# Moving one aggregation step, making M later, and giving the last pair its own end in a GCN and graph-attention kernel

## The chip, the cores and the metric

The kernel runs on one core of one Trainium2 chip. The metric is device time in microseconds (us). Before the change the median of three runs is 2903.5 us (2902.86 to 2904.16). Engine names follow the profile: PE is TensorE, DVE is VectorE, ACT is ScalarE, POOL is GpSimd, SP is SyncE, whose queue issues all DMAs here.

## The reference

There are 64 graphs with 256 nodes and 512 features, all in fp32. Layer 0 is a three-layer GCN with a residual and a layernorm; layer 1 is an attention that gates each node's value vector by a softmax over the nodes of its graph.

```python
def _gcn_layer(x, adj, W, b):
    return adj @ (x @ W) + b                      # per graph
h = relu(_gcn_layer(x, adj, W1, b1)); h = relu(_gcn_layer(h, adj, W2, b2))
x = layernorm(x + _gcn_layer(h, adj, W3, b3))
q, k = split(x @ Wqk, 2); v = x @ Wv
w = mask / sqrt(512) * sum(q * (adj @ (k * mask)), axis=-1)
x = layernorm(x + softmax(w over nodes)[:, :, None] * v)
```

## The kernel before, in words

**Pairs.** Two graphs make a pair, so there are 32 pairs. Nodes are split in two halves of 128 (`h`), features in four chunks of 128 (`c`).

**Seven products.** Every large multiplication apart from the aggregation is done with seven block products in place of eight. `seven` (L96 to L131) fixes their order: 1, 7, 6, 2, 5, 3, 4. Products 1, 6, 5 and 3 accumulate one after another in the same PSUM bank x, product 7 and then 4 in bank v, and 2 has its own bank y. Between them ACT copies the bank out (L103 after 1, L112 after 6, L120 after 5) and DVE adds a bank and a copy into a result block (L62). So product 6 may not start before the copy after 1 is done, product 5 not before the copy after 6, product 3 not before the copy after 5, and product 4 not before DVE's add "c22", which reads the copy after 5 and bank v.

**Sums for the products.** The products need sums of blocks. `a_sums` builds four from one operand on POOL (L65): first S[2] (for product 7), then S[0] (for 5), S[1] (for 6, made from S[0]), S[3] (for 3, made from S[1]). `b_sums` (L87 to L90) does it for the other operand: on DVE for the weights, on POOL for T and for M.

**Front of a pair (F).** `support` (L231) multiplies activations by W with seven products; `aggregate` (L252) multiplies by the adjacency in four steps of four matmuls, one for each feature chunk in the order 2, 3, 0, 1, and ACT evicts each with ReLU (L255). This is done for W1 and W2, then `support` for W3. After the first `support` the transposed x of the next pair is loaded (L70); the plain x of this pair is loaded after the second aggregation (L80).

**Back of a pair (B).** `adj_times` (L284) applies the adjacency (first gather), the residual and the layernorm follow: ACT makes the masked xm (L385), DVE normalises r (L387) and transposes it in 32x32 blocks (L390); the result goes to DRAM (L393) and comes back with four DMAs (L395) as x1T, which completes the transpose. A second gather multiplies adjacency by xm (L284 again, sums on POOL). Then `attention(g)` for each of the two graphs: seven products (L412) of x1T and its sums (POOL, L65) with Wv and with M = Wq Wk^T side by side, 512 columns wide, and the scores on DVE (L416). The text calls these seven products together the double product.

**Making M.** `make_m` loads Wq, Wk and Wv (L181 to L186), multiplies them in four rows of 16 matmuls (L192, copied by ACT L195) and builds the sums mv_T on POOL (L87 to L90).

**Finish of a pair (E).** Softmax of both graphs together: two PE transposes (L305), maximum (L307), exponential on ACT with an activation table load (L310), two transposes back (L319), then gating (L446), bn_stats and aggregate (L453, L457), square root (L294, another table load), normalisation (L462) and the output DMAs, one per graph (L465).

**Order of the work.** Nothing is reordered by a scheduler: each engine runs its instructions as the program issues them. F, B and E are generators; `run` advances them by a string, one letter for each step. Iteration i runs F of pair i, B of pair i-1 and E of pair i-2. `ORDER` is that string for i of 1 and more; iteration 0 uses "FB" six times; the last pair's E runs alone at the end. Buffers with few copies matter: S has 11, v (attention result) 2, x, r, gt, x1T and xT one each, PSUM 8 banks.

Of the kernel before, what the change touches and what calls it, by code (L numbers as in the profile page):

```python
# [9 lines left out]
FP = mybir.dt.float32  # L10
AF = mybir.ActivationFunctionType
# [9 lines left out]
def gcn_then_graph_attention(ctx: ExitStack, tc: tile.TileContext, xT, xN, adjT, mask, W1, b1, W2, b2, W3, b3,  # L21
# [33 lines left out]
    def bank(shape=(P, G, N)):  # L55
        return psum.tile(list(shape), FP, name="ps", tag="ps")
# [4 lines left out]
    def add(o, a, b):  # L61
        nc.vector.tensor_tensor(o, a, b, op=OP.add)  # L62

    def padd(o, a, b, op=OP.add):
        nc.gpsimd.tensor_tensor(o, a, b, op=op)  # L65
# [134 lines left out]
        yield  # L200


    def a_sums(blk, part=None):


        S = [pool.tile([P, 2, G, P], FP, name="S", tag="S", bufs=11) for _ in range(4)]
        sub = OP.subtract

        def first():
            padd(S[2], blk(0, 0), blk(1, 0), sub)  # L210

        def rest():
            padd(S[0], blk(1, 0), blk(1, 1))
            padd(S[1], S[0], blk(0, 0), sub)

        def last():
            padd(S[3], blk(0, 1), S[1], sub)
# [55 lines left out]
    def t_sums(B):  # L273
        Ts = [pool.tile([P, G, HD], FP, name="T", tag="T", bufs=4) for _ in range(4)]
        b_sums((B[0][0], B[0][1], B[1][0], B[1][1]), Ts, nc.gpsimd)
        return Ts

    def adj_times(aS, B, Ts, c11, c12, c21, c22, plus=None):

        mov = {1: B[0][0], 2: B[1][0], 3: B[1][1], 4: Ts[3], 5: Ts[0], 6: Ts[1], 7: Ts[2]}  # L280

        def mm(n, ps, first):
            for g in range(G):
                nc.tensor.matmul(ps[:, g], lhsT=aS[n][:, g], rhs=mov[n][:, g], start=(first and g == 0),  # L284
                                 stop=(g == G - 1), skip_group_check=True)
        yield from seven(mm, (P, G, HD), c11, c12, c21, c22, plus=plus)

    def row_stats(st, src):
        nc.vector.bn_stats(st, src)

    def inv_std(mvt):

        sd = small.tile([P, NH, G], FP, name="sd")
        nc.scalar.activation(sd, mvt[:, :, :, 1], AF.Sqrt, bias=eps)  # L294
        rs = small.tile([P, NH, G], FP, name="rs")
        nc.vector.reciprocal(rs, sd)
        nb = small.tile([P, NH, G], FP, name="nb")
        nc.vector.scalar_tensor_tensor(nb, mvt[:, :, :, 0], -1.0, rs, op0=OP.mult, op1=OP.mult)
        return rs, nb

    def softmax_rows(w):

        pw = bank((G, N))
        for h in range(NH):
            nc.tensor.transpose(pw[:, h * P:(h + 1) * P], w[:, h, :], ident)  # L305
        nmax = small.tile([G, 1], FP, name="nmax")
        nc.vector.tensor_reduce(nmax, pw, AX.X, OP.max, negate=True)  # L307
        e = small.tile([G, N], FP, name="e", bufs=1)
        tot = small.tile([G, 1], FP, name="tot")
        nc.scalar.activation(e, pw, AF.Exp, bias=nmax, accum_out=tot)  # L310
        rtot = small.tile([G, 1], FP, name="rtot")
# [4 lines left out]
    def softmax_cols(sm):  # L316
        ps = bank((P, NH, G))
        for h in range(NH):
            nc.tensor.transpose(ps[:, h, :], sm[:, h * P:(h + 1) * P], ident[:G, :G])  # L319
        s = small.tile([P, NH, G], FP, name="s", bufs=2)  # L320
        nc.vector.tensor_copy(s, ps)
        return s

# [27 lines left out]
        C = yield from steps  # L351
        return C, aS, x, nxt, nS

    def back(i, C, aS, x):
        Ts = t_sums(C)
        r = pool.tile([P, G, NH, D], FP, name="r", bufs=1)
        xb = lambda h, j: x[:, :, h, j * HD:(j + 1) * HD]
# [23 lines left out]
        tr = pool.tile([P, 4, 32, NH, 2, 2, G], FP, name="tr", tag="gt", bufs=1)  # L381
        x1T = pool.tile([P, P, NH, 2, 2, G], FP, name="x1T", bufs=1)
        for h in range(NH):
            for g in range(G):
                nc.scalar.activation(xm[:, g, h, :], r[:, g, h, :], AF.Identity, scale=mrs[:, h, g:g + 1],  # L385
                                     bias=mnb[:, h, g:g + 1])
                nc.vector.tensor_scalar(r[:, g, h, :], r[:, g, h, :], rs[:, h, g:g + 1], nb[:, h, g:g + 1],  # L387
                                        op0=OP.mult, op1=OP.add)
# [3 lines left out]
        via = dram.tile([4, P, D], FP, name="via")  # L392
        nc.sync.dma_start(via.rearrange("q p e -> p q e"), tr.rearrange("p q j h k c g -> p q (j h k c g)"))  # L393
        for q in range(4):
            nc.sync.dma_start(x1T[q * 32:(q + 1) * 32].rearrange("p (a j) h k c g -> p a (j h k c g)", a=4),  # L395
                              via[q].rearrange("(a i) e -> i a e", a=4))
        yield
        xmb = [[xm[:, :, h, j * HD:(j + 1) * HD] for j in range(2)] for h in range(2)]
        Ts = t_sums(xmb)
# [6 lines left out]
        def attention(g):  # L406
# [12 lines left out]
            def c22(ps, t):  # L419
# [5 lines left out]
        yield from adj_times(aS, xmb, Ts, lambda y, t: add(gb(0, 0), y, t), lambda x: nc.scalar.copy(gb(0, 1), x),  # L425
                             lambda v, t: add(gb(1, 0), v, t), lambda v, t: add(gb(1, 1), v, t))
        if i + 2 < NPAIR:
            aTs[i + 2] = load_adj(i + 2)
        src, first, rest, last = a_sums(lambda h, k: x1T[:, :, h, k].rearrange("p n c g -> p c g n"))
        first()  # L430
        rest()
        last()
# [2 lines left out]
            yield from attention(g)  # L435
        return r, vs, w

    def finish(i, prev):

        r, vs, w = prev  # L440
        sm = softmax_rows(w)
        yield
        s = softmax_cols(sm)
        for g in range(G):
            for h in range(NH):
                nc.vector.scalar_tensor_tensor(vs[g][:, h, :], vs[g][:, h, :], s[:, h, g:g + 1], r[:, g, h, :],  # L446
                                               op0=OP.mult, op1=OP.add)
        yield
        st = small.tile([P, NH, G, 6], FP, name="st")
        mvt = small.tile([P, NH, G, 2], FP, name="mvt")  # L450
        for g in range(G):
            for h in range(NH):
                nc.vector.bn_stats(st[:, h, g], vs[g][:, h, :])  # L453
                yield
        for g in range(G):
            for h in range(NH):
                nc.vector.bn_aggr(mvt[:, h, g], st[:, h, g])  # L457
        rs, nb = inv_std(mvt)
        yield
        for g in range(G):  # L460
            for h in range(NH):
                nc.scalar.activation(vs[g][:, h, :], vs[g][:, h, :], AF.Identity, scale=rs[:, h, g:g + 1],  # L462
                                     bias=nb[:, h, g:g + 1])
# [23 lines left out]
    for i in range(NPAIR + 1):  # L487
        gens = {}
        if i < NPAIR:
            aT = aTs[i]  # L490
            gens["F"] = front(i, xTs, xS, aT)
        if i == 0:
            gens["B"] = make_m()
        else:
            gens["B"] = back(i - 1, *state)
        if prev is not None:
            gens["E"] = finish(i - 2, prev)
        res = run(ORDER.replace(" ", "") if i else "FB" * 6, **gens)
# [42 lines left out]
```

## Time and profile before

| what | value |
|---|---|
| median of three runs | 2903.5 us |
| the profiled execution's own time | 2903.94 us |
| its span, first to last instruction | 2902.1 us |
| mean granted TensorE clock | 0.995 |
| busy, DVE / ACT / POOL | 39% / 32% / 49% |
| one iteration in the steady state (from one long "issue" piece of the chain to the next) | 88.31 us |

The profiled execution took 1.84 us more than its span. A page of the profile gives busy times by engine, the span in 40 slices, and groups of instructions by line; the timeline lists instructions in order of time with the start, the duration, the form, and in brackets the idle time of the engine before it and what ended it. Matmuls of fp32 appear as two records for each instruction (a "x8" is four matmuls), and their listed durations overlap, so the starts are what counts.

### The profile page before, as it was taken

What the parts mean: (1) busy time and instruction counts of PE and PEld (TensorE: products, weight loads), DVE (VectorE), ACT (ScalarE), POOL (GpSimd) and SP (SyncE); (2) the same over time, 40 slices, a digit from 0 to 9 for tenths busy, and PEclk for the clock granted to TensorE, in tenths of its full rate; (3) what the DMA queues carried; (4) which work ended last, traced back from release to release, by engine and by line L of the source; (5) the groups of instructions that cost most, each with busy time, mean ns of one, the idle gap of its engine ahead of it and who ended that gap; (6) DMA issues with size and microseconds to landing.
All of it is one profiled execution on the core that took longest, in us unless ns stands there. A gap on an engine that the chain in (4) does not pass through costs nothing.

```text
span 2902.1 us, 29670 instructions
## 1 busy us (share of the span) xinstructions
PE 2828.6 (97%) x11264; PEld 2174.2 (75%) x11264; DVE 1123.4 (39%) x2318; ACT 934.1 (32%) x1510; POOL 1432.1 (49%) x1130
## 2 busy tenths in 40 slices
PE   7999999999999999999999999999999999999995
PEld 6877777777777777777777777777777777777773
DVE  1243334443344433344433444433444333444334
ACT  1323333322333332333223333323332333332232
POOL 2644554354554455553545544545534455435452
PEclk9999999999999999999999999999999999999998
DMA  4211222212222112222122221122221122221111
GB/s 150 66 41 54 66 80 80 60 43 66 72 80 80 44 51 66 80 80 73 39 64 66 80 80 51 44 66 80 80 80 41 54 66 81 80 60 45 56 58 58
DMA packets 64046, 193.10 MB, mean 67 GB/s; under 512 B 5792, under 2 KB 8992, under 8 KB 55712
## 3 DMA queue, kind: packets, MB, share of 16 engines
q1 hardware_dynamic: 63904, 191.19, 21.1%
q8 instruction: 90, 1.47, 0.2%
q14 instruction: 52, 0.43, 0.0%
HBM read 124.06 MB, written 67.11 MB: 66 GB/s over the span
## 4 chain that ended last, share of the span: by engine, by line
PE 65%; issue 17%; POOL 14%; ACT 1%; DMA 1%; DVE 1%; SPq 0%; POOLq 0%; ACTq 0%
PE ps L231 27%; PE ps L412 25%; POOL S L65 8%; PE ps L284 7%; PE ps L252 6%; POOL T L88 2%; POOL T L89 1%; POOL T L87 1%; POOL T L90 1%; ACT hT L255 1%; PE ps L192 1%; DMA w<-in_W 0%; PE ps L319 0%; PE ps L305 0%; DMA wkT<-in_WkT 0%
## 5 line engine op out<-in xcount | busy, mean ns | idle before, releaser
L231 PE MATMUL ps<-w_T,S 128*128 128x256 f32 x2304 | 548.8, 381 | 1.4 <-DVE w_T L87 1.1
L231 PEld LDWEIGHTS ps<-w_T,S 128*128 128x128 f32 x2304 | 433.7, 191 | 106.2 <-issue 51.0
L252 PE MATMUL ps<-aT,sup 128*128 128x256 f32 x2048 | 467.6, 379 | 0.0
L65 POOL TENSOR_TENSOR S<-hT 128x512 f32<-128x512 f32 x128 | 162.4, 1269 | 601.1 <-ACT hT L255 601.1
L252 PEld LDWEIGHTS ps<-aT,sup 128*128 128x128 f32 x2048 | 389.2, 190 | 66.0 <-issue 14.8
L62 DVE TENSOR_TENSOR sup<-ps,tmp 128x512 f32<-128x512 f32 x288 | 198.7, 690 | 509.4 <-PE ps L231 262.6
L412 PE MATMUL ps<-mv_T,S 128*128 128x512 f32 x768 | 367.1, 601 | 27.3 <-POOL S L65 27.3
L65 POOL TENSOR_TENSOR tmp<-tmp,x 128x512 f32<-128x512 f32 x96 | 120.3, 1268 | 485.9 <-ACT tmp L120 295.2
L62 DVE TENSOR_TENSOR v<-ps,tmp 128x512 f32<-128x512 f32 x128 | 88.5, 692 | 692.7 <-PE ps L412 692.7
L255 ACT ACTIVATE hT<-ps,b 128x512 f32<-128x512 f32 x256 | 175.3, 685 | 392.3 <-PE ps L252 392.3
L112 ACT COPY tmp<-ps 128x512 f32<-128x512 f32 x224 | 131.2, 586 | 496.9 <-PE ps L231 219.6
L412 PEld LDWEIGHTS ps<-mv_T,S 128*128 128x128 f32 x768 | 140.7, 190 | 187.9 <-issue 115.3
L103 ACT COPY tmp<-ps 128x512 f32<-128x512 f32 x224 | 129.8, 580 | 410.5 <-PE ps L231 235.9
L120 ACT COPY tmp<-ps 128x512 f32<-128x512 f32 x224 | 131.1, 585 | 374.5 <-PE ps L412 185.3
L412 PE MATMUL ps<-v,x1T 128*128 128x512 f32 x512 | 240.9, 593 | 2.8 <-DMA x1T<-via 2.8
L231 PE MATMUL ps<-w,hT 128*128 128x256 f32 x1024 | 241.9, 379 | 0.0
L231 PEld LDWEIGHTS ps<-w,hT 128*128 128x128 f32 x1024 | 194.6, 190 | 49.7 <-issue 22.2
L284 PE MATMUL ps<-T,aS 128*128 128x256 f32 x768 | 203.4, 388 | 2.1 <-POOL T L87 1.4
L231 PE MATMUL ps<-w,S 128*128 128x256 f32 x768 | 186.4, 386 | 1.5 <-ACT tmp L120 1.5
L231 PEld LDWEIGHTS ps<-w,S 128*128 128x128 f32 x768 | 140.6, 190 | 47.2 <-issue 25.7
L412 PEld LDWEIGHTS ps<-v,x1T 128*128 128x128 f32 x512 | 141.3, 295 | 41.8 <-issue 3.6
L65 POOL TENSOR_TENSOR x<-x,b3b 128x512 f32<-128x512 f32 x128 | 172.1, 1373 | 0.0
(96 smaller groups left out, 3869.8 us busy)
## 6 DMA issues: line engine op xcount, KB each, us to landing
xT<-in_xT SPq DMA_DIRECT2D x32, 1024.0 KB, 4.9
x<-in_xN SPq DMA_DIRECT2D x32, 1024.0 KB, 6.5
via<-tr SPq DMA_DIRECT2D x32, 1024.0 KB, 4.3
x1T<-via SPq DMA_DIRECT2D x128, 256.0 KB, 4.7
out<-v SPq DMA_DIRECT2D x64, 512.0 KB, 3.6
aT<-in_adjT SPq DMA_DIRECT2D x32, 512.0 KB, 3.6
w<-in_W SPq DMA_DIRECT2D x9, 256.0 KB, 5.2
wqT<-in_WqT SPq DMA_DIRECT2D x4, 256.0 KB, 6.1
```

Source lines behind the costliest of these rows:

```text
L62: nc.vector.tensor_tensor(o, a, b, op=OP.add)
L65: nc.gpsimd.tensor_tensor(o, a, b, op=op)
L87: eng.tensor_tensor(Ts[2], B[3], B[1], op=sub)
L88: eng.tensor_tensor(Ts[0], B[1], B[0], op=sub)
L103: nc.scalar.copy(t1, x)
L112: nc.scalar.copy(u, x)
L120: nc.scalar.copy(q, x)
L231: nc.tensor.matmul(ps[:, g], lhsT=src[n][:, c, g], rhs=w[n][:, c], start=(first and g == 0 and c == 0), stop=(g == G - 1 and c == 1), skip ...
L252: nc.tensor.matmul(ps[:, g], lhsT=C[k][c // 2][:, g, (c % 2) * P:(c % 2 + 1) * P], rhs=aT[:, k, g], start=(g == 0 and k == 0), stop=(g == ...
L255: nc.scalar.activation(hT[c // 2][:, c % 2], ps, AF.Relu, bias=b[:, c:c + 1])
L284: nc.tensor.matmul(ps[:, g], lhsT=aS[n][:, g], rhs=mov[n][:, g], start=(first and g == 0), stop=(g == G - 1), skip_group_check=True)
L412: nc.tensor.matmul(ps, lhsT=src[n][:, c, g], rhs=mv[n][:, c], start=(first and c == 0), stop=(c == 1), skip_group_check=True)
```

## The change

1. `ORDER` is rewritten. In every steady iteration one F step, the fourth step of the second aggregation (chunk 1), moves from behind product 7 to ahead of it: PE's order was "1, 7, aggregation step, 6" and is now "1, aggregation step, 7, 6". The later F steps are spread anew between the products of the two graphs, and E's last steps come a place earlier, so that both output DMAs are issued ahead of the load of x.
2. Iteration 0 runs twelve F steps first and then F and B in turn, so the rows of M stand between the products of the second `support`, not of the first. On SP's queue the load of the next pair's xT then stands ahead of the loads of Wq, Wk and Wv.
3. The last pair has its own end. Its r is transposed by 16 TensorE transposes into four PSUM banks, which DVE (first half) and ACT (second half) copy to x1T; the two DRAM passes are gone. Its a_sums run on DVE. The second gather (G) and the first graph's products (M) are interleaved as "GMGMGMGMGGGMMM". The softmax and the finish are done for each graph by itself: the first graph's between the second graph's products, the second's at the end. The steps of E of the pair before are spread over this end by a string of their own.

The rest is parameters: `a_sums` takes an engine, `inv_std`, `softmax_rows`, `softmax_cols` and `finish` take a number or list of graphs. The call of `a_sums` for x1T stands ahead of the second gather in the program, but its instructions are issued where they were.

```diff
-    def a_sums(blk, part=None):
+    def a_sums(blk, eng=nc.gpsimd):
...
-            padd(S[2], blk(0, 0), blk(1, 0), sub)
+            eng.tensor_tensor(S[2], blk(0, 0), blk(1, 0), op=sub)
...
-    def back(i, C, aS, x):
+    def back(i, C, aS, x, end):
...
+        if end:
+            x1T = pool.tile([P, 2, 2, G, N], FP, name="x1T", bufs=1)
+            x1b = lambda h, k: x1T[:, k, :, :, h * P:(h + 1) * P]
+            for h, g in hg:
+                apply(h, g)
+            Ts = t_sums(xmb)
+            for h, g in hg:
+                pt = bank((P, 2, 2, P))
+                for c in range(DC):
+                    nc.tensor.transpose(pt[:, c // 2, c % 2], r[:, g, h, c * P:(c + 1) * P], ident)
+                (nc.scalar.copy if h else nc.vector.tensor_copy)(x1T[:, :, :, g, h * P:(h + 1) * P], pt)
+        else:
...
+        src, first, rest, last = a_sums(x1b, nc.vector if end else nc.gpsimd)
+        if end:
+            first()
+            rest()
+            last()
+            one = attention(0)
+            for k in "GMGMGMGMGGGMMM":
+                next(gather if k == "G" else one)
+                yield
...
+            tail = finish(i, (r, vs, w), [0])
+            for _ in attention(1):
+                next(tail, None)
+                yield
+            for _ in tail:
+                pass
+            for _ in finish(i, (r, vs, w), [1]):
+                pass
+            return
+        yield from gather
...
-    ORDER = ("F E F" + " B F" + " B F E" * 5 + " B F B F F B B F F B F" + " B F" * 3 + " B F E" * 4 + " E B" +
-             (" B F" * 2 + " B" + " B F" * 3 + " B") * 2)
+    ORDER = ("F E F" + " B F" + " B F E" * 5 + " B F B F F B B F F B F" + " B F"*3 + " B F E"*3 + " B E F E" + " B F E B B F B B F B F B" + " B F B B F B B F B F B")
+    START = "F" * 12 + "F B" * 6
+    END = "E B B B E" + "B" * 5 + "B E" * 10
...
-    for _ in finish(NPAIR - 1, prev):
-        pass
```

More of the change, by code (lines that the diff above doesn't have):

```diff
@@ L209, in first @@
         def first():
-            padd(S[2], blk(0, 0), blk(1, 0), sub)
+            eng.tensor_tensor(S[2], blk(0, 0), blk(1, 0), op=sub)
         def rest():
-            padd(S[0], blk(1, 0), blk(1, 1))
-            padd(S[1], S[0], blk(0, 0), sub)
+            eng.tensor_tensor(S[0], blk(1, 0), blk(1, 1), op=OP.add)
+            eng.tensor_tensor(S[1], S[0], blk(0, 0), op=sub)
         def last():
-            padd(S[3], blk(0, 1), S[1], sub)
+            eng.tensor_tensor(S[3], blk(0, 1), S[1], op=sub)
         return {1: blk(0, 0), 2: blk(0, 1), 4: blk(1, 1), 5: S[0], 6: S[1], 7: S[2], 3: S[3]}, first, rest, last
@@ L286, in adj_times, with inv_std, softmax_rows @@
         yield from seven(mm, (P, G, HD), c11, c12, c21, c22, plus=plus)
[L288 to L293, printed above, removed]
+    def inv_std(mvt, n=G):
+        sd = small.tile([P, NH, n], FP, name="sd")
         nc.scalar.activation(sd, mvt[:, :, :, 1], AF.Sqrt, bias=eps)
-        rs = small.tile([P, NH, G], FP, name="rs")
+        rs = small.tile([P, NH, n], FP, name="rs")
         nc.vector.reciprocal(rs, sd)
-        nb = small.tile([P, NH, G], FP, name="nb")
+        nb = small.tile([P, NH, n], FP, name="nb")
         nc.vector.scalar_tensor_tensor(nb, mvt[:, :, :, 0], -1.0, rs, op0=OP.mult, op1=OP.mult)
         return rs, nb
-    def softmax_rows(w):
-        pw = bank((G, N))
+    def softmax_rows(w, gs):
+        n = len(gs)
+        pw = bank((n, N))
         for h in range(NH):
-            nc.tensor.transpose(pw[:, h * P:(h + 1) * P], w[:, h, :], ident)
-        nmax = small.tile([G, 1], FP, name="nmax")
+            nc.tensor.transpose(pw[:, h * P:(h + 1) * P], w[:, h, gs[0]:gs[0] + n], ident)
+        nmax = small.tile([n, 1], FP, name="nmax")
         nc.vector.tensor_reduce(nmax, pw, AX.X, OP.max, negate=True)
-        e = small.tile([G, N], FP, name="e", bufs=1)
-        tot = small.tile([G, 1], FP, name="tot")
+        e = small.tile([n, N], FP, name="e", bufs=1)
+        tot = small.tile([n, 1], FP, name="tot")
         nc.scalar.activation(e, pw, AF.Exp, bias=nmax, accum_out=tot)
-        rtot = small.tile([G, 1], FP, name="rtot")
+        rtot = small.tile([n, 1], FP, name="rtot")
         nc.vector.reciprocal(rtot, tot)
@@ L314, in softmax_rows, with softmax_cols @@
         return e
-    def softmax_cols(sm):
-        ps = bank((P, NH, G))
+    def softmax_cols(sm, gs):
+        n = len(gs)
+        ps = bank((P, NH, n))
         for h in range(NH):
-            nc.tensor.transpose(ps[:, h, :], sm[:, h * P:(h + 1) * P], ident[:G, :G])
-        s = small.tile([P, NH, G], FP, name="s", bufs=2)
+            nc.tensor.transpose(ps[:, h, :], sm[:, h * P:(h + 1) * P], ident[:n, :n])
+        s = small.tile([P, NH, n], FP, name="s", bufs=2)
         nc.vector.tensor_copy(s, ps)
@@ L380, in back, with apply @@
         xm = pool.tile([P, G, NH, D], FP, name="xm", tag="x", bufs=1)
[L381 to L388, printed above, removed]
+        def apply(h, g):
+            nc.scalar.activation(xm[:, g, h, :], r[:, g, h, :], AF.Identity, scale=mrs[:, h, g:g + 1],
+                                 bias=mnb[:, h, g:g + 1])
+            nc.vector.tensor_scalar(r[:, g, h, :], r[:, g, h, :], rs[:, h, g:g + 1], nb[:, h, g:g + 1],
+                                    op0=OP.mult, op1=OP.add)
+        hg = [(h, g) for h in range(NH) for g in range(G)]
+        xmb = [[xm[:, :, h, j * HD:(j + 1) * HD] for j in range(2)] for h in range(2)]
+        if end:
[10 more added lines that the diff above has]
+        else:
+            tr = pool.tile([P, 4, 32, NH, 2, 2, G], FP, name="tr", tag="gt", bufs=1)
+            x1T = pool.tile([P, P, NH, 2, 2, G], FP, name="x1T", bufs=1)
+            x1b = lambda h, k: x1T[:, :, h, k].rearrange("p n c g -> p c g n")
+            for h, g in hg:
+                apply(h, g)
                 for k in range(2):
@@ L391, in back @@
                                         r[:, g, h, k * HD:(k + 1) * HD].rearrange("p (c q j) -> p c q j", c=2, q=4))
[L392 to L399, printed above, removed]
+            via = dram.tile([4, P, D], FP, name="via")
+            nc.sync.dma_start(via.rearrange("q p e -> p q e"), tr.rearrange("p q j h k c g -> p q (j h k c g)"))
+            for q in range(4):
+                nc.sync.dma_start(x1T[q * 32:(q + 1) * 32].rearrange("p (a j) h k c g -> p a (j h k c g)", a=4),
+                                  via[q].rearrange("(a i) e -> i a e", a=4))
+            yield
+            Ts = t_sums(xmb)
         yield
@@ L424, in attention @@
                              lambda ps, t: add(v[:, 1, :], ps, t), c22)
-        yield from adj_times(aS, xmb, Ts, lambda y, t: add(gb(0, 0), y, t), lambda x: nc.scalar.copy(gb(0, 1), x),
-                             lambda v, t: add(gb(1, 0), v, t), lambda v, t: add(gb(1, 1), v, t))
+        gather = adj_times(aS, xmb, Ts, lambda y, t: add(gb(0, 0), y, t), lambda x: nc.scalar.copy(gb(0, 1), x),
+                           lambda v, t: add(gb(1, 0), v, t), lambda v, t: add(gb(1, 1), v, t))
+        src, first, rest, last = a_sums(x1b, nc.vector if end else nc.gpsimd)
[7 more added lines that the diff above has]
+                yield
+            for _ in gather:
+                pass
+            for _ in one:
+                pass
+            tail = finish(i, (r, vs, w), [0])
+            for _ in attention(1):
+                next(tail, None)
+                yield
+            for _ in tail:
+                pass
+            for _ in finish(i, (r, vs, w), [1]):
+                pass
+            return
+        yield from gather
         if i + 2 < NPAIR:
             aTs[i + 2] = load_adj(i + 2)
-        src, first, rest, last = a_sums(lambda h, k: x1T[:, :, h, k].rearrange("p n c g -> p c g n"))
         first()
@@ L436, in back, with finish @@
         return r, vs, w
-    def finish(i, prev):
+    def finish(i, prev, gs=range(G)):
         r, vs, w = prev
-        sm = softmax_rows(w)
+        n = len(gs)
+        sm = softmax_rows(w, gs)
         yield
-        s = softmax_cols(sm)
-        for g in range(G):
+        s = softmax_cols(sm, gs)
+        for k, g in enumerate(gs):
             for h in range(NH):
-                nc.vector.scalar_tensor_tensor(vs[g][:, h, :], vs[g][:, h, :], s[:, h, g:g + 1], r[:, g, h, :],
+                nc.vector.scalar_tensor_tensor(vs[g][:, h, :], vs[g][:, h, :], s[:, h, k:k + 1], r[:, g, h, :],
@@ L447, in finish @@
                                                op0=OP.mult, op1=OP.add)
         yield
-        st = small.tile([P, NH, G, 6], FP, name="st")
-        mvt = small.tile([P, NH, G, 2], FP, name="mvt")
-        for g in range(G):
+        st = small.tile([P, NH, n, 6], FP, name="st")
+        mvt = small.tile([P, NH, n, 2], FP, name="mvt")
+        for k, g in enumerate(gs):
             for h in range(NH):
-                nc.vector.bn_stats(st[:, h, g], vs[g][:, h, :])
+                nc.vector.bn_stats(st[:, h, k], vs[g][:, h, :])
@@ L454, in finish @@
                 yield
-        for g in range(G):
+        for k in range(n):
             for h in range(NH):
-                nc.vector.bn_aggr(mvt[:, h, g], st[:, h, g])
-        rs, nb = inv_std(mvt)
+                nc.vector.bn_aggr(mvt[:, h, k], st[:, h, k])
+        rs, nb = inv_std(mvt, n)
         yield
-        for g in range(G):
+        for k, g in enumerate(gs):
             for h in range(NH):
-                nc.scalar.activation(vs[g][:, h, :], vs[g][:, h, :], AF.Identity, scale=rs[:, h, g:g + 1],
-                                     bias=nb[:, h, g:g + 1])
+                nc.scalar.activation(vs[g][:, h, :], vs[g][:, h, :], AF.Identity, scale=rs[:, h, k:k + 1],
+                                     bias=nb[:, h, k:k + 1])
@@ L494, in gcn_then_graph_attention @@
         else:
-            gens["B"] = back(i - 1, *state)
+            gens["B"] = back(i - 1, *state, i == NPAIR)
         if prev is not None:
             gens["E"] = finish(i - 2, prev)
-        res = run(ORDER.replace(" ", "") if i else "FB" * 6, **gens)
+        order = START if i == 0 else ORDER if i < NPAIR else END
+        res = run(order.replace(" ", ""), **gens)
         if i > 0:
```

## The prediction

> **What bounds the kernel.** First the page: busy times, then the slices.
>
> ```profile
> PE 2828.6 (97%) x11264; PEld 2174.2 (75%) x11264; DVE 1123.4 (39%) x2318; ACT 934.1 (32%) x1510; POOL 1432.1 (49%) x1130
> ...
> PE   7999999999999999999999999999999999999995
> ```
>
> PE is the bound in every slice but the first and the last. The change removes no matmul, so it can only win what PE idles: in the steady state, at the start, at the end. Second, the timeline of PE and then POOL in one steady iteration (start, duration, form, idle time before it):
>
> ```profile
> 1196.01 1.88 PE L412 MATMUL ps<-v,x1T 128*128 128x512 f32 x4
> 1198.72 1.98 PE L412 MATMUL ps<-mv_T,S 128*128 128x512 f32 x4 [0.82 <-POOL S L65]
> 1200.54 1.89 PE L252 MATMUL ps<-aT,sup 128*128 128x256 f32 x8
> 1202.27 1.98 PE L412 MATMUL ps<-mv_T,S 128*128 128x512 f32 x4
> ```
>
> ```profile
> 1195.25 1.27 POOL L65 TENSOR_TENSOR S<-hT 128x512 f32<-128x512 f32 x1 [12.26 <-ACT hT L255]
> 1196.48 4.12 POOL L65 TENSOR_TENSOR S<-x1T 128x512 f32<-128x512 f32 x2
> 1200.68 1.52 POOL L65 TENSOR_TENSOR S<-S,x1T 128x512 f32<-128x512 f32 x1
> ```
>
> The four PE rows are product 1, product 7, the aggregation step and product 6. Product 7 waits for S[2], POOL's first sum of x1T; this is the largest wait of an iteration (27.3 us in all, 33 times). Counted from starts it is 1198.72 - 1196.01 - 1.72 (a product back to back) = 0.99. Note when S[1] is done: 1200.68 + 1.52 = 1202.20, and product 6, which reads it, starts at 1202.27.
>
> Third, the first 30 us on PE:
>
> ```profile
> 11.64 3.75 PE L231 MATMUL ps<-w_T,S 128*128 128x256 f32 x8 [1.11 <-DVE w_T L87]
> 21.36 6.28 PE L192 MATMUL ps<-wkT,wqT 128*128 128x128 f32 x32 [5.96 <-DMA wkT<-in_WkT]
> 29.20 3.73 PE L192 MATMUL ps<-wkT,wqT 128*128 128x128 f32 x32
> ```
>
> PE idles 5.96 us for the weights of M. The first two rows are also slow: product 7 takes 3.55 from start to end against 1.73 later, and the first row of M 6.1 against 3.57. The rows become fast at 26.4, 5.0 us into unbroken work. (The stage table gives a granted clock of 1.00 here and 0.52 for 2847 to 2853; its records come late, so I go by the starts of rows.)
>
> Fourth, the end:
>
> ```profile
> 2840.53 2.08 PE L284 MATMUL ps<-xm,aT 128*128 128x256 f32 x4 [6.13 <-ACT xm L385]
> 2846.74 0.37 SPq L393 DMA_DIRECT2D via<-tr  x1
> 2851.14 1.74 SPq L395 DMA_DIRECT2D x1T<-via  x4
> 2857.83 2.06 PE L412 MATMUL ps<-v,x1T 128*128 128x512 f32 x4 [2.80 <-DMA x1T<-via]
> 2863.63 1.98 PE L412 MATMUL ps<-mv_T,S 128*128 128x512 f32 x4 [1.55 <-POOL S L65]
> 2889.28 2.74 DVE L446 SCALAR_TENSOR_TENSOR v<-v,s,r 128x512 f32<-128x512 f32 x4
> 2895.50 2.93 ACT L462 ACTIVATE v<-v,nb,rs 128x512 f32<-128x512 f32 x4 [0.49 <-DVE nb L298]
> ```
>
> With no front beside it, the double product starts only when x1T is back from DRAM (2857.83), waits for POOL's sums, and after its last matmul (2886.28) both graphs' softmax and finish stand alone, 15.82 us.
>
> **Part 1, the moved step: nothing.** POOL's order of instructions is unchanged, and its chain starts at the same event: ACT's eviction of the aggregation's second step (1195.25). So S[1] is still ready at 1202.20. New PE order: product 1 at 1196.01, the step at 1197.73, product 7 at 1199.45 (S[2], ready at 1198.67, no longer holds it), done at 1201.17. Product 6 then waits for S[1] until 1202.25. Before, it started at 1202.27. The wait of 0.99 goes and one of 1.08 comes, one product later. I take -0.02 x 31 = -0.6 us, with ends of -3 and +3 (0.1 an iteration, the size of a restart after a wait in these rows).
>
> The steps spread anew: every product keeps at least one other product (1.72) between itself and the copy it needs, which takes about 0.9 (0.2 to start, 0.58 to copy, 0.06 back). The products 4 now have three between. DVE and ACT do the same work within a few us. T's sums on POOL start some 3.4 us later (product 3 of the front is two places later), at about 1230.7, and are needed at 1241.3: hidden. On SP both outputs now precede the load of x: the issue moves from 1196.35 to about 1198.8, it lands 6.5 later, and POOL reads x at 1210.41: hidden, with 5 us to spare.
>
> **Part 2, M later: -6.3.** The time to compare is the first product of pair 1, at 87.62. After: product 6 follows product 7 at 15.19. With the 5.0 us of above the slow stretch ends at 16.6, and the 1.5 us of it beyond 15.19 cost half, 0.8: 17.7. Products 2, 5, 3, 4 take 4 x 1.73, and 0.93 for the copy ahead of product 3 (as at 63.82): 25.6. Aggregation 6.91: 32.5. Products 1, 7 and 6 with 0.3 for S[1]: 37.9. Four rows of M (3.57 each) with three products: 57.4. Now POOL's sums for M come later against the front by one product: they start 0.87 after the last row and take 9.47, as before (44.24 to 53.71), until 67.7. PE has product 4, aggregation and product 1 until 67.7, then waits for the third support's S[2] and S[1], queued on POOL behind them: product 6 at 71.6 (3.89 after, as at 57.60). This wait is 2.2 in place of 0.4. From there 9.74 as before: 81.3. The eight loads for M now queue on SP behind the load of xT, which waits for product 4 (25.8). It lands at about 30.7, and at the 0.68 us between landings in this trace the eight are in by 36.1, 1.8 before the first row. If that cover goes, each us late is a us lost. Ends: -7 (no slow stretch beyond 15.19) to -1 (loads up to 5 late).
>
> **Part 3, the last end: -9.3.**
> - Up to the layernorm (xm starts at 2839.66): E's bn_stats no longer stand among DVE's residual adds; one (0.66) was on the path, and its neighbours: -0.95, so 2838.7.
> - r follows ACT tile by tile (0.85 behind, 0.7 apart), then 16 transposes. The trace has no 128x128 transpose; the nearest rows are L305, two columns wide and warm (0.109 each), and L192, slow (0.213 a record, and 0.427 with two records). I take 0.213, since one transpose is one record in L305 and the clock is low: 2840.15 to 2843.55. Ends 1.7 and 6.9 in all. The copies to x1T cost 0.58 and 0.69 each (L112, L62), DVE's four sums 0.69 each as in L88, up to 1.60 where POOL works beside (L87 at 9.89); S[2] by 2846 at worst, needed at about 2849: hidden.
> - Second gather 7 x 0.86 and first graph 7 x 1.72 interleaved: 18.1. Slow clock: no row tells whether transposes count as work that ends the slow stretch, so I count its 5.0 us from halfway, 2841.9; 3.4 us of the block are slow and cost 1.7 (ends 0 and 9.0, all of it slow). Waits: 0.9 twice, where product 3 follows 5 directly, and 0.5 where DVE's c11 of the first graph waits for a v buffer, whose output DMA is issued only after ACT's normalisation in this stretch (2.7 to land); queued behind it on DVE is the gather's c22, for which product 4 waits. End at 2865.6; the second graph started at 2873.32: -7.7.
> - Second graph: 12.0, 0.9 for product 3, and PE's queue now holds the first graph's softmax: the transposes back stand ahead of product 6 and wait for an activation table load (1.28) behind ACT's copy, 1.4 in all, plus 0.5 for the transposes. It ends at 2880.5 (before 2886.28).
> - The finish of one graph in place of two: L446 -1.38, L453 -1.23, L457 -0.18, L462 -1.47; another 0.7 is lost as the exponential's table load now stands behind the first graph's normalisation. 15.82 becomes 12.3: 2892.8 against 2902.1.
>
> [...]
>
> **The sum.** 2902.1 - 0.6 - 6.3 - 9.3 = 2885.9; plus 1.84 around the span 2887.7, and the median stands 0.4 under the profiled execution: 2887.5.
>
> **Rivals.**
> 1. The steady wait vanishes wholly: 31 x 1.1 = 34 less, 2854. For it: product 7's wait is the one the profile names. Against it: S[1] at 1202.20. It needs POOL's chain to start about 1 us earlier. 5%.
> 2. The ends give little: the clock stays low through the interleaved stretch (9.0 in place of 1.7), or the rows of M wait for their loads (up to 6, as now). 2894 to 2901. For it: 2840 to 2852 is slow now. Against it: PE then had gaps of 1.4 and 0.75, and now has none. 10%.
> 3. Slower: PSUM. Product 1 of the second graph now follows product 4 of the first directly and needs a fresh bank. If none of the eight is free it waits for DVE's score, about 0.9, in every iteration: 31 x 0.9 = 28, 2915. It decides from the ninth bank; I count six in use there. 4%.
> 4. Forecast: 81%.
>
> **How the numbers follow.** The forecast's range comes from the ends above: 2881 to 2897. A measurement of this kernel can tell about 0.2% (5.8 us) from no change. Faster (under 2897.7): 5 + 81 and some 4 of rival 2, 0.90; same 0.06; slower 0.04.
>
> **What would show it.** Part 1: product 6 waits about 1.1 for POOL S, product 7 not at all, and an iteration takes 88.3; a period under 87.5 proves part 1 wrong. Part 2: pair 1's first product near 81, M's first row without a DMA wait. Part 3: no via DMA after the last front, x1T ready by 2838, and about 12 us from the last 128x512 product to the end. A cold clock beyond 15 us in the end, or a new wait in every iteration, would make the prediction wrong.

## The result and the profile after

The changed kernel takes 2885.48 us (median of four runs, 2885.23 to 2885.68) against 2903.18 (2902.7 to 2904.16): a ratio of 0.9939, 95% interval 0.9921 to 0.9956, or 17.7 us less. The forecast was 2887.5. The profiled execution of after took 2885.68 us with a span of 2883.9, so 18.2 of span went:

| stretch | before | after | difference | forecast |
|---|---|---|---|---|
| up to the first product of pair 1 | 87.62 | 78.70 | -8.9 | -6.3 |
| the 31 iterations from there to the softmax of pair 30 on PE (a steady one: 88.31, then 88.33) | 2737.1 | 2737.5 | +0.4 | -0.6 |
| from that softmax to the span's end | 77.4 | 67.7 | -9.7 | -9.3 |

The rows that bound the stretches, two of before and two of after:

```profile
87.62 1.89 PE L231 MATMUL ps<-w,xT 128*128 128x256 f32 x8
2824.69 0.38 PE L305 MATMUL ps<-ident,w 128*2 128x128 f32 x2
```

```profile
78.70 1.89 PE L232 MATMUL ps<-w,xT 128*128 128x256 f32 x8
2816.18 0.38 PE L304 MATMUL ps<-ident,w 128*2 128x128 f32 x2
```

Line numbers move: in after, the products of the attention are L428 (L412 before), the sums of `a_sums` L211 to L218 (L65), `support` L232, the gathers L285. The page of after, busy time and slices:

```profile
PE 2821.4 (98%) x11284; PEld 2174.5 (75%) x11284; DVE 1130.0 (39%) x2322; ACT 938.8 (33%) x1517; POOL 1426.2 (49%) x1126
...
PE   8999999999999999999999999999999999999996
```

On PE only the first and the last slice changed. PE's busy time fell by 7.2 us though it has 20 more records: fewer of its rows run at the slow clock (slow up to 26.58 and from 2840.53 to 2853.04 in before, up to 12.88 and from 2825.30 to 2835.57 in after; mean granted clock 0.995, then 0.997). Now one steady iteration of after, PE and then POOL (start, duration, form, idle time before it and what ended it):

```profile
1187.25 1.88 PE L428 MATMUL ps<-v,x1T 128*128 128x512 f32 x4
1188.97 1.89 PE L253 MATMUL ps<-aT,sup 128*128 128x256 f32 x8
1190.70 1.88 PE L428 MATMUL ps<-mv_T,S 128*128 128x512 f32 x4
1193.54 1.98 PE L428 MATMUL ps<-mv_T,S 128*128 128x512 f32 x4 [0.96 <-POOL S L215]
```

```profile
1186.49 1.28 POOL L211 TENSOR_TENSOR S<-hT 128x512 f32<-128x512 f32 x1 [12.26 <-ACT hT L256]
1187.72 2.19 POOL L211 TENSOR_TENSOR S<-x1T 128x512 f32<-128x512 f32 x1
1189.87 2.02 POOL L214 TENSOR_TENSOR S<-x1T 128x512 f32<-128x512 f32 x1
1191.96 1.52 POOL L215 TENSOR_TENSOR S<-S,x1T 128x512 f32<-128x512 f32 x1
```

The aggregation step stands ahead of product 7, product 7 (1190.70) no longer waits, and product 6 does, by its start 1193.54 - 1190.70 - 1.72 = 1.12. It waits for S[1], done at 1191.96 + 1.52 = 1193.48. POOL's rows stand as before, and their chain still begins when ACT releases the sum of hT.

The start of after:

```profile
10.34 4.87 PE L232 MATMUL ps<-w_T,S 128*128 128x256 f32 x16
15.04 1.89 PE L232 MATMUL ps<-w,xT 128*128 128x256 f32 x8
...
35.27 3.73 PE L192 MATMUL ps<-wkT,wqT 128*128 128x128 f32 x32
...
66.40 1.99 PE L232 MATMUL ps<-w_T,S 128*128 128x256 f32 x8 [1.12 <-POOL S L211]
68.96 1.99 PE L232 MATMUL ps<-w_T,S 128*128 128x256 f32 x8 [0.57 <-POOL S L215]
```

The first row of M is at full speed (3.73, where before took 6.28) and waits for no DMA. The price of M's later sums is in the last two rows, in the third `support`. And the end of after, from the transposes on:

```profile
2831.46 2.82 PE L398 MATMUL ps<-ident,r 128*128 128x128 f32 x12 [5.07 <-DVE r L385]
2834.71 1.02 PE L398 MATMUL ps<-ident,r 128*128 128x128 f32 x4 [0.43 <-DVE r L385]
2835.57 1.03 PE L285 MATMUL ps<-xm,aT 128*128 128x256 f32 x4
...
2847.60 1.13 PE L285 MATMUL ps<-xm,aS 128*128 128x256 f32 x4 [0.67 <-ACT tmp L120]
2849.77 1.10 PE L285 MATMUL ps<-T,aT 128*128 128x256 f32 x4 [1.04 <-DVE gt L62]
...
2856.80 1.88 PE L428 MATMUL ps<-v,x1T 128*128 128x512 f32 x4
...
2861.83 0.28 PE L319 MATMUL ps<-ident,e 1*128 1x1 f32 x2 [1.21 <-DVE e L312]
...
2871.72 0.38 PE L304 MATMUL ps<-ident,w 128*1 128x128 f32 x2
2874.57 0.28 PE L319 MATMUL ps<-ident,e 1*128 1x1 f32 x2 [2.47 <-DVE e L312]
```

x1T no longer comes from DRAM. Right after the last transposes the gather runs at full speed in this run (2835.57, 1.03 for four records; before, the same row took 2.08). The second graph starts at 2856.80, its last product ends at 2871.72, and 12.2 us later the span ends.

### The profile page after: what moved, and what is told of

Same layout as the page of the kernel before. It is cut to its first block, busy times and chain, and to the rows that moved or that the text cites. A ratio compares the mean times of both kernels' runs of the same rounds, so it can differ in the third digit from the quotient of the medians.

```text
span 2883.9 us, 29739 instructions
## 1 busy us (share of the span) xinstructions
PE 2821.4 (98%) x11284; PEld 2174.5 (75%) x11284; DVE 1130.0 (39%) x2322; ACT 938.8 (33%) x1517; POOL 1426.2 (49%) x1126
## 4 chain that ended last, share of the span: by engine, by line
PE 62%; POOL 18%; issue 17%; ACT 1%; DVE 1%; DMA 0%; POOLq 0%; ACTq 0%; SPq 0%; DVEq 0%
PE ps L232 27%; PE ps L428 23%; PE ps L285 7%; PE ps L253 4%; POOL S L211 4%; POOL S L214 4%; POOL S L215 3%; POOL T L88 2%; POOL T L89 1%; POOL T L87 1%; POOL T L90 1%; POOL S L218 1%; ACT hT L256 1%; PE ps L192 0%; PE ps L319 0%
## 5 line engine op out<-in xcount | busy, mean ns | idle before, releaser
L232 PE MATMUL ps<-w_T,S 128*128 128x256 f32 x2304 | 548.2, 381 | 1.7 <-POOL S L211 1.1
L232 PEld LDWEIGHTS ps<-w_T,S 128*128 128x128 f32 x2304 | 433.9, 191 | 106.2 <-issue 51.4
L428 PE MATMUL ps<-mv_T,S 128*128 128x512 f32 x768 | 359.2, 597 | 29.1 <-POOL S L215 29.1
L211 POOL TENSOR_TENSOR S<-hT 128x512 f32<-128x512 f32 x64 | 81.4, 1272 | 536.0 <-ACT hT L256 536.0
L65 POOL TENSOR_TENSOR tmp<-tmp,x 128x512 f32<-128x512 f32 x96 | 120.4, 1269 | 432.1 <-ACT tmp L120 293.3
L428 PEld LDWEIGHTS ps<-mv_T,S 128*128 128x128 f32 x768 | 143.4, 190 | 188.5 <-issue 121.9
L232 PE MATMUL ps<-w,hT 128*128 128x256 f32 x1024 | 241.9, 379 | 0.0
L428 PE MATMUL ps<-v,x1T 128*128 128x512 f32 x512 | 240.7, 593 | 0.0
L232 PEld LDWEIGHTS ps<-w,hT 128*128 128x128 f32 x1024 | 194.7, 190 | 49.5 <-issue 22.2
L285 PE MATMUL ps<-T,aS 128*128 128x256 f32 x768 | 200.4, 383 | 0.3 <-ACT tmp L103 0.3
L87 POOL TENSOR_TENSOR T<-sup 128x512 f32<-128x512 f32 x32 | 40.4, 1264 | 309.3 <-ACT sup L234 309.3
L232 PE MATMUL ps<-w,S 128*128 128x256 f32 x768 | 186.4, 386 | 1.5 <-ACT tmp L120 0.8
L428 PEld LDWEIGHTS ps<-v,x1T 128*128 128x128 f32 x512 | 141.8, 291 | 46.9 <-issue 2.9
L232 PEld LDWEIGHTS ps<-w,S 128*128 128x128 f32 x768 | 140.8, 190 | 46.9 <-issue 25.6
```

The source lines that it names most:

```text
L211: eng.tensor_tensor(S[2], blk(0, 0), blk(1, 0), op=sub)
L232: nc.tensor.matmul(ps[:, g], lhsT=src[n][:, c, g], rhs=w[n][:, c], start=(first and g == 0 and c == 0), stop=(g == G - 1 and c == 1), skip ...
L428: nc.tensor.matmul(ps, lhsT=src[n][:, c, g], rhs=mv[n][:, c], start=(first and c == 0), stop=(c == 1), skip_group_check=True)
```

## Experiments

### The three parts, each alone

e1 is the kernel before with the new order of steps in pairs 1 to 31 only; e2 is it with the new start only; e3 is the changed kernel with the old order and the old start, so with the new end only.

```diff
 e1: -  run(ORDER ... if i else "FB" * 6, **gens)
     +  run((MOVED if i < NPAIR else ORDER) ... if i else "FB" * 6, **gens)
 e2: -  ... if i else "FB" * 6, **gens)
     +  ... if i else "F" * 12 + "FB" * 6, **gens)
 e3: -  ORDER = (new), START = "F" * 12 + "F B" * 6
     +  ORDER = (old), START = "FB" * 6
```

> The kernel before with the new order of steps for pairs 1 to 31 alone (no change at the start, none at the end). Theory (the wait moves from product 7 to product 6 because POOL's S[1] is ready at the same time): the period stays at 88.31 to 88.34 us, PE waits about 1.0 us for POOL's S in product 6 in place of product 7, and the time is that of before, +0 to +1 us. Rival (the moved step covers the wait): the period falls to about 87.2 and the time by 31 x 1.1 = 34 us.

> The kernel before with M made later and nothing else. Theory: the first product of pair 1 moves from 87.6 to between 78.7 (as in the changed kernel) and 81.3 (as worked out in the prediction), and the time falls by 6 to 9 us. Rival (the rows of M wait for loads that now stand behind xT): a DMA wait before the first row of M, and a gain under 4 us.

> The kernel before with the new end of the last pair alone. Theory: the 77.4 us from the softmax of pair 30 to the end of the span become 67.7, as in the changed kernel, and the time falls by 9 to 10 us; e1, e2 and e3 together add up to the whole gain of 17.7 within 1.5 us. Rival (the parts depend on one another, for instance through the phase of the clock): the sum misses the whole by more than 2 us.

| run | median us | against before (2902.94) | ratio, interval |
|---|---|---|---|
| e1, order only | 2903.50 | +0.6 | 1.0001 [0.9992, 1.0010] |
| e2, start only | 2894.99 | -7.95 | 0.9972 [0.9961, 0.9983] |
| e3, end only | 2892.70 | -10.2 | 0.9963 [0.9951, 0.9976] |

The sum, -17.6, is the whole change (-17.7): the medians give no sign that the parts touch one another. e3 is just above the 9 to 10 expected. e1's waits of PE, from the table of waits (waiting instruction, releaser: us in all, times, longest):

```profile
PE ps L412 <- POOL S L65: 29.2, 32, 0.9
```

Its timeline tells which product waits:

```profile
1201.82 1.98 PE L412 MATMUL ps<-mv_T,S 128*128 128x512 f32 x4 [0.94 <-POOL S L65]
```

This is product 6; product 7 (1199.00) follows the aggregation step without a wait. The kernel before had 27.3 us in 33 waits there. So the first part of the change moved the wait from product 7 to product 6 and took nothing from it.

### The sums of x1T ahead in POOL's queue

If POOL's chain sets the wait, its sums have to be queued earlier, not the products later. In `ORDER` one B step is the one that issues the four sums of x1T. e4 is the changed kernel with this B step placed one F step earlier, ahead of the second aggregation's second step (chunk 3). That step issues POOL's sum of hT, and the sum waits for ACT's eviction in the same step. e5 does the same to the kernel before, with its old order, start and end.

```diff
 the steps around it, letters of ORDER, [SUMS] the B step that issues the sums of x1T
-  F(chunk 3) [SUMS] F(chunk 0) ...      POOL: S<-hT (waits for ACT), S<-x1T x4
+  [SUMS] F(chunk 3) F(chunk 0) ...      POOL: S<-x1T x4, S<-hT
```

> The changed kernel with one letter of the order moved: the step that issues POOL's four sums of x1T stands ahead of the aggregation step whose eviction POOL waits for 12 us, so POOL makes S[2], S[0], S[1], S[3] of x1T as soon as x1T has landed, some 3 us earlier. Theory (POOL's queue, not PE's order, sets the wait): PE waits for POOL's S in neither product, the period falls from 88.33 to about 87.15 (1.08 of waiting and a restart of 0.1), and the time to 2885.5 - 31 x 1.18 = 2849. Rival (another wait of the same size stands behind it): the period stays above 88 and another releaser is named.

> The kernel before, with its old order of F steps, its old start and its old end; only the back's step that issues the sums of x1T comes one F step earlier in pairs 1 to 31. Theory (the wait belongs to POOL's queue, where the x1T sums stood behind a sum that waits for ACT; the place of the aggregation step is worth nothing): the period falls from 88.31 to 87.1 us as in the variant with the new order, 31 x 1.2 = 37 less, about 2866, and no PE wait for POOL's S is left in the steady state. Rival (the moved step is what makes room, and both are needed): product 7 still follows product 1 directly and waits a part of the time, the period stays above 87.5, the time above 2878.

e4: **2848.23 us** (2847.96 to 2849.34), ratio 0.9811 [0.9798, 0.9825]. e5: 2867.09 (2865.86 to 2867.5), ratio 0.9875 [0.9861, 0.9888]. Their periods are 87.12 (88.33 in after) and 87.13 (88.31 in before). POOL and PE of e4:

```profile
1168.60 2.18 POOL L211 TENSOR_TENSOR S<-x1T 128x512 f32<-128x512 f32 x1 [9.17 <-DMA x1T<-via]
...
1172.83 1.53 POOL L215 TENSOR_TENSOR S<-S,x1T 128x512 f32<-128x512 f32 x1
...
1175.91 1.26 POOL L211 TENSOR_TENSOR S<-hT 128x512 f32<-128x512 f32 x1
```

```profile
1172.45 1.88 PE L428 MATMUL ps<-v,x1T 128*128 128x512 f32 x4
1174.17 1.89 PE L253 MATMUL ps<-aT,sup 128*128 128x256 f32 x8
1175.90 3.60 PE L428 MATMUL ps<-mv_T,S 128*128 128x512 f32 x8
```

Products 7 and 6 are now one row of eight records without a wait: S[1] is done at 1174.36, 3.3 us before product 6 needs it (1177.6). POOL had been idle for 9.17 us until x1T landed; in after it was idle for 12.26 us and x1T had been there for 3.1 of them (landed 1183.37). The chain that ended last tells the same at a glance, shares of the span by engine, first after, then e4:

```profile
PE 62%; POOL 18%; issue 17%; ACT 1%; DVE 1%; DMA 0%; POOLq 0%; ACTq 0%; SPq 0%; DVEq 0%
```

```profile
PE 98%; POOL 1%; DVE 1%; ACT 0%; issue 0%; DMA 0%; ACTq 0%; SPq 0%; POOLq 0%
```

e5 has product 7 directly behind product 1, as before, and gains as much (36.6 us in medians; by periods 31 x 1.19 = 36.9). The place of the aggregation step is worth nothing with the old queue (e1) and nothing with the new one (e5 against e4).

### Does a transpose raise the clock?

e6 adds 22 transposes of the identity on PE to e4, before the kernel's first product; e7 adds 11 matmuls of the identity by itself in their place. The results are read by nobody.

```diff
+    warm = bank((P, 4, P))
+    for k in range(22):
+        nc.tensor.transpose(warm[:, k % 4], ident, ident)
```

> The variant with the early sums, and 22 transposes of the identity on PE between 1.4 us and about 6.6 us, before the first product of the kernel (6.8 us). Theory (transposes count as work that ends the slow stretch, as the last end of the changed kernel suggests): the first product, 3.75 us for its eight records without them, takes about 1.9. Rival (they do not count): it still takes 3.75. The time itself should stay within 1 us of the variant without them, 2848.2, since the second product waits for a sum of W1 on DVE (ready at 10.1) either way.

> The same with 11 matmuls of the identity by itself (128 columns) in place of the 22 transposes: by both theories the first product takes about 1.9 us for its eight records, if about 5 us of unbroken work end the slow stretch. If it stays at 3.75, then the stretch of work was too short, and the run with transposes tells nothing either. The time stays near 2848.

One run each: 2847.95 and 2848.41 us, the time of e4, as expected. The first rows of e6:

```profile
1.36 4.96 PE L171 MATMUL ps<-ident 128*128 128x128 f32 x22 [1.36 <-POOL ident masks.py:199]
6.74 1.97 PE L235 MATMUL ps<-w,xT 128*128 128x256 f32 x8 [0.42 <-DMA w<-in_W]
10.27 1.97 PE L235 MATMUL ps<-w_T,S 128*128 128x256 f32 x8 [1.57 <-DVE w_T L87]
```

and of e7:

```profile
6.81 1.97 PE L235 MATMUL ps<-w,xT 128*128 128x256 f32 x8 [0.55 <-DMA w<-in_W]
```

The first product takes 1.97 in both; without them it takes 3.75, in before, after, e2 and e8 alike. So 22 transposes ended the slow stretch here as 11 matmuls did. The trace's record of the granted clock says the same: in e6 it goes to full at 6.34, counted from the start of the span, before any product has started. The last row of e6 tells why nothing is won: product 7 waits for a sum of W1 until 10.27 either way.

The new end points the same way, though the row behind the transposes is not fast in every run. In e4 it is slow:

```profile
2797.91 1.91 PE L285 MATMUL ps<-xm,aT 128*128 128x256 f32 x4
```

The granted clock rises 1.8 us after the start of this row in e4, 1.3 after it in e3 and 0.6 in e6. In after, e7, e8 and e9 it rises up to 0.4 us ahead of it. Counted from the first transpose, it rises after 3.4 us (e9) to 5.9 us (e4). Most of that stretch is transposes in every run.

### Two small waits

e8 is e4 with the sums for M on DVE, and with both graphs' v of the last pair in the buffer of xT, which no load needs any more.

```diff
-        b_sums((v0, m[0], v1, m[1]), ts, nc.gpsimd)
+        b_sums((v0, m[0], v1, m[1]), ts, nc.vector)
...
+        vend = pool.tile([P, DC, G, N], FP, name="xT", bufs=1) if end else None
...
-            v = pool.tile([P, NH, D], FP, name="v", tag="v", bufs=2)
+            if end:
+                v = vend[:, 2 * g:2 * g + 2].rearrange("p c a n -> p c (a n)")
+            else:
+                v = pool.tile([P, NH, D], FP, name="v", tag="v", bufs=2)
```

> The variant with the early sums, with two more edits: the four sums for M are made on DVE, not on POOL, and in the last pair both graphs' v lie in the buffer of xT, which is free by then. Theory: the two waits of the third support (1.12 and 0.57 us) go, so pair 1's first product starts at 76.7 in place of 78.4; in the end the wait of the gather's product 4 (1.04) goes, so the end from the softmax of pair 30 takes 66.8 in place of 67.9. Together 2.7 less than 2848.2: 2845.5. Rival: DVE's sums of M (0.7 to 1.6 each) stand ahead of the adds that the front's products 4 wait for, and POOL works beside them: pair 1's first product stays at 78, and only the end gains: 2847.

**2845.22 us** (2844.49 to 2846.05), ratio 0.9800 [0.9787, 0.9813]: the fastest version here. e4 and e8 stood beside different runs of before, and 3 us is about what such a comparison can tell; the traces show it better. Of e8:

```profile
63.09 1.89 PE L232 MATMUL ps<-w,hT 128*128 128x256 f32 x8
64.82 3.89 PE L232 MATMUL ps<-w_T,S 128*128 128x256 f32 x16
...
76.46 1.89 PE L232 MATMUL ps<-w,xT 128*128 128x256 f32 x8
...
2807.97 1.13 PE L285 MATMUL ps<-xm,aS 128*128 128x256 f32 x4 [0.68 <-ACT tmp L120]
2808.94 1.03 PE L285 MATMUL ps<-T,aT 128*128 128x256 f32 x4
```

The third support's products 7 and 6 are one row (pair 1 starts at 76.46 against 78.36 in e4), and the gather's product 4 follows product 3 after 0.97, in place of 2.17 in after and 1.42 in e4. The end takes 66.4 against 67.7 in after and 67.9 in e4 (66.8 was expected). After is the fairer comparison for the buffer, 1.3 us: like e8 it has a fast row behind the transposes. Against e4, 1.0 of the gain is there before the gather's product 3 starts, since e4's rows behind the transposes are slow.

### The end taken apart

e9 is the changed kernel with one softmax and finish for both graphs of the last pair; e10 is it with r sent through DVE's transposes and DRAM as before, the gather first.

```diff
 e9:  -            for _ in attention(1):
      -                next(tail, None)
      -                yield
      ...
      +            for _ in attention(1):
      +                yield
      +            for _ in finish(i, (r, vs, w)):
      +                pass
 e10: -        if end:
      -            x1T = ... (transposes on TensorE)
      -        else:
      -            tr = ...
      +        tr = ... (for every pair)
      ...
      -            for k in "GMGMGMGMGGGMMM":
      +            for k in "GGGGGGGMMMMMMM":      (sums of x1T ahead of the first M)
```

> The changed kernel with one part of its end undone: the last pair's softmax and finish are done for both graphs together, after the last product. Theory (the separate finish wins what the prediction says and pays for it in the second graph's products): the second graph's products take 12.9 us in place of 14.9, since no transposes and no wait for the exponential stand between them, and the finish 15.8 in place of 12.2: 1.6 more, 2887.1. Rival (the work of the first graph's finish costs nothing between the products): the whole 3.6 comes back, 2889.1.

> The changed kernel with another part of its end undone: r of the last pair goes through DVE's 32x32 transposes and DRAM as before, the whole second gather first, then the sums of x1T (on DVE) and both graphs; the separate softmax stays. Theory (the transposes and the interleaving win what x1T's way through DRAM costs): from xm to the first graph's first product it takes 18.2 us as in the kernel before, so that product starts at 2848.2 and the first graph is done at about 2861 in place of 2856.8; with up to 2 us more of slow clock, since PE is idle for some 10 us: 2890 to 2891.5. Rival (the gather covers the passes through DRAM): within 1 us of 2885.5.

e9: 2887.10 us (2886.83 to 2887.39), ratio 0.9945 [0.9933, 0.9958]. In its trace the second graph takes 12.96 (2856.24 to 2869.20) and the finish 15.8: the theory's two terms. The separate finish is worth 1.6 us, not the 3.6 of the rival. One row of it bears on the clock, the last four transposes, 0.70 in place of 1.02 in after:

```profile
2834.15 0.70 PE L398 MATMUL ps<-ident,r 128*128 128x128 f32 x4 [0.43 <-DVE r L385]
```

e10: 2892.78 us (2891.97 to 2893.15), ratio 0.9965 [0.9951, 0.9978], 7.3 more than the changed kernel, above the 4.5 to 6 expected. Its trace:

```profile
2843.70 1.03 PE L285 MATMUL ps<-T,aT 128*128 128x256 f32 x4
2848.18 3.71 PE L416 MATMUL ps<-v,x1T 128*128 128x512 f32 x4 [3.46 <-DMA x1T<-via]
2851.72 3.60 PE L416 MATMUL ps<-mv_T,S 128*128 128x512 f32 x8
```

The first product starts at 2848.18 (2848.2 expected) and is slow, 3.71 in place of 1.88. Counted from the softmax of pair 30, the first graph is done 6.3 later than with transposes, and the second graph takes 0.3 more (PE waits 1.58 for the first graph's exponential, 1.21 in after). The two profiled executions differ by 6.6, the medians by 7.3; the 0.7 between them is within what two comparisons can tell. Of the 6.3, 1.8 is the slow first product (3.54 to the next start in place of 1.72). In the kernel before the clock was full at that place (full from 2852.79; the same row took 2.06), so this much of e10's loss goes by the clock. Whether the way through DRAM brings it about is not shown: PE had idled 3.46 us there, and 2.80 in before. e10 also keeps the sums of x1T on DVE: behind its first product nothing waits for them, where the kernel before waited 0.54 and 1.82 by starts for POOL's.

## Why the prediction was right, and where its terms were off

**Part 1, the moved step, worth nothing: right.** +0.4 us over 31 iterations, e1 +0.6, where -0.6 with ends of 3 was said. The step that carried it, that S[1] is ready at the same moment whatever PE does, holds: product 6 waits 1.12 (1.08 said). Rival 1 named its own condition, that POOL's chain would have to start about 1 us earlier. e4 and e5 fulfil it, and 37 us go (34 said). That rival was not a matter of chance: it is another edit.

**Part 2, M later: mechanism right, -6.3 too small.** Measured -8.9 between the two profiled executions and -7.95 in medians (e2), both beyond its own end of -7. From product 2 of the first support to pair 1 the working gave 81.3 - 17.7 = 63.6, and 78.70 - 15.04 = 63.7 came. It includes M's first row without a DMA wait and the waits for POOL's sums of M, 2.1 by starts where 2.2 was said; e8 shows that these are the price of sums on POOL. The mis-sized term stands ahead of product 2: 17.7 said, 15.04 measured. I let product 7 start at 11.64 as in the profiled execution of before, where the sum of W1 started at 9.89, took 1.60 beside POOL's work and ended at 11.49. That varies from run to run: product 7 started at 11.52 in e5, at 10.3 to 10.5 in after and in the other runs without a warm-up (in after the sum started at 9.12, took 1.07 and ended at 10.19). In these two traces it goes with which of POOL's sums is running when W1 lands: the fourth, until 10.95, in before; the third, until 9.64, in after. And I counted the slow stretch anew from product 7, so until 16.6. The rows of after run from 6.78 without a break and become fast at 12.88. The earlier start is worth 1.3 of the 2.7, the shorter slow stretch 1.4.

**Part 3, the end: -9.7 against -9.3, with two terms that were added and in fact overlap.**

| step, us after the softmax of pair 30 | said | measured |
|---|---|---|
| first transpose starts | 15.5 | 15.3 |
| transposes done | 18.9 | 19.4 |
| first graph done | 40.9 | 40.6 |
| second graph's last product done | 55.8 | 55.5 |
| end of the span | 68.1 | 67.7 |

A transpose cost 0.213 as taken, but the last four wait 0.43 for the last tile of r, whose normalisation on DVE took 1.59 beside POOL's sums (0.55 for the other three). After them the clock is fast in after, so the 1.7 for slow rows is 0 there; the wait for a v buffer is 1.3 by starts where 0.5 was said, and e8 removes it with another buffer. The other two waits of 0.9 are there as said (0.84 each).

That these two errors nearly cancel is no chance. In e4, e3 and e6 the rows behind the transposes are slow for 1.8, 1.3 and 0.6 us. Yet the gather's product 4, which stands behind the wait for the v buffer, starts 33.6 to 33.7 us after the softmax of pair 30 in all six runs with this buffer (after, e3, e4, e6, e7, e9). Only its distance from product 3 changes, from 1.42 in e4 to 2.28 in e9. The output DMA that frees the buffer lands 32.0 us after that softmax in after, e3, e6 and e7 and 32.2 in e4, and DVE's add starts 0.1 later. So this DMA sets the start of product 4, and slow rows ahead of it cost next to nothing; in e8, with another buffer, it is 32.3. The working added the slow rows and the wait one behind the other.

No row of before told whether transposes end the slow stretch, and the working counted its 5.0 us from halfway through them. These runs tell it: in e9 the last four of 16 fp32 transposes are already faster (0.70, and 1.02 in after), in after the matmul behind them runs at full speed (1.03 against 2.08 in before), and e6 shows it by itself (1.97 against 3.75). The time of the end, -9.7, does not decide it, since slow rows are hidden here; the spacing of the rows does.

**The rivals.** The ends giving little: no; both parts came whole (e2, e3). PSUM: product 1 of the second graph follows without a wait (2856.80), and the period grew by 0.02, not by 0.9. e9 and e10 tell in part what the end consists of: the transposes with the interleaving are worth some 7 against e10, of which 1.8 is e10's slow product; the separate finish is worth 1.6; and xm starts 1.14 earlier against the softmax of pair 30, the residual adds having no bn_stats between them. That these add up to 9.7 hides two things that nearly cancel: e10's slow product, and the kernel before's waits for POOL's sums in the first graph (2.4 by starts), which DVE's sums remove in e10 too. No run tried DVE's sums alone.

**Two readings of the working.** It calls the records of the granted clock late. They are not (see the last section). And the lower end of the range, 2881, is the sum of the lower ends, but the upper ends add up to 2907, or to 2900 without the 9.0 that is rival 2's, and not to 2897.

## What to carry to other kernels

Here the waiting engine's instructions were reordered and the producer's queue was not, and the wait moved on to the next consumer (27.3 us in 33 waits before, 29.2 in 32 in e1); ask of the producer what stands ahead in its queue and what that waits for. Here POOL, which took its sums in the order of issue, was idle for 12.26 us ahead of a sum whose operand came late, while the operand of the next four sums had been there for 3.1; one letter in the order of issue was worth 37 us, twice the whole change. At the two ends of a kernel, where nothing covers a wait, every microsecond of the chain counts, but a finish split in two paid part of its gain back between the products: 1.6 of 3.6 us stayed (e9).

## What the runs showed of the hardware

- The slow stretch at the start of PE's work had no fixed length in these runs. From the first row to the first fast one it took 5.2 us in before (21.36 to 26.58), 4.1 for the same rows in e3 (20.30 to 24.4), 6.1 in after (6.78 to 12.88), 3.7 in the end of e8 (2791.94 to 2795.65). A constant of 5.0 from one place was a poor term. The changes of the granted clock stand whole multiples of 3.41 us apart in the traces of before and after: in before the low stretch of the end lasts 17.07 us (5 times 3.41) and the full one behind it 37.55 (11 times), in after 10.24 (3 times) and 40.96 (12 times). In e10 the shortest low stretch lasts 3.41.
- The records of the granted clock agree with the spacing of the rows. The trace's time of the first record of before is 37.44, but the span starts at 10.89 on the same scale, so it stands at 26.55; the rows become fast at 26.58. At the end of before the clock goes back to full at 2852.79 and the rows are fast from 2853.04; in after it does so at 12.72 and 2835.54, and the rows at 12.88 and 2835.57. The 1.00 that the stage table gives for the first 26 us of before is no measurement: no record lies there.
- Some DVE operations took longer where a POOL sum ran beside them. The product of the scores that reads tmp (L416 before, L432 after) took 1.37 to 1.44 in the 31 of 64 cases of each trace in which it began while a POOL sum ran, and 0.75 in the other 33; the one that reads PSUM took 0.75 to 0.76 in all 64, and 62 of them began beside a POOL sum. In the end of after the normalisation took 0.55 and 1.59 (0.46 to 0.90 in the other 124, which all began beside a POOL sum), a sum of x1T 0.69 and 1.75. Where a DVE sum of two SBUF blocks began while a POOL sum ran, it ended 0.54 to 0.56 us after that POOL sum: 11.49 against 10.95 in before, 10.19 against 9.64, 2837.59 against 2837.04 and 2839.27 against 2838.71 in after. The product that reads tmp ended 0.55 after the POOL sum in all the 31 cases of each trace.
